# Layer 1's gate projection by seven block products for every eight, with VectorE and ScalarE carrying the partial sums

## The chip, the cores and the metric

The kernel runs on one core of a Trainium2 chip. The metric is the device time of one execution in microseconds (us), lower being better: the median of several runs. The time before is 768.36 us, the median of three runs from 768.17 to 768.40. One core has five engines that matter here, each with an instruction queue of its own: TensorE (PE in the profile, its weight loads are PEld), VectorE (DVE), ScalarE (ACT), GpSimd (POOL) and SyncE (SP), which issues the DMAs.

## The reference, cut to what matters

Two layers work on x, 4 x 512 x 256 in float32. Layer 0 (an mLSTM block, and a feed-forward part with routed low-rank experts) is the same before and after. Layer 1 is:

```python
xn = layernorm(x)
# attention over the four batch entries, causal among them, 16 heads of 16
q, k, v = split(einsum('lne,fe->lnf', xn, weight_qkv), 3)
attn = softmax(where(causal, (q * 16**-0.5) @ k, -inf))
a = (attn @ v) @ weight_out.T
# gated feed-forward part, of every four values the two largest are kept
h = silu(xn @ w_gate) * (xn @ w_up)          # w_gate and w_up: 256 x 1024
f = sparsify_2to4(h) @ w_down
out = x + a + f
```

The attention's sequence is the first axis of x (length 4, B in the code), and it is causal: position l = 0 sees itself alone, so its result is its own v whatever its q is.

## The kernel before

The 512 positions are cut into four row blocks (j = 0 to 3, NJ = 4) of 128 positions for each of the 4 batch entries; a row block is thus 512 rows, and its normed rows lie transposed in `xnT`, two tiles of 128 x 512 (k = 0, 1, the halves of the 256 features).

What layer 1 does for one row block:

- `front_rows(j)`: layernorm statistics on VectorE, one power on GpSimd (`rstd`), the norm on VectorE (`xn`), eight TensorE transposes (`pt`), two ScalarE copies into `xnT`.
- `attention_rows(j)`: for each l, TensorE forms q and k in one product of 512 columns (`qk_ps`) and v in one of 256 (`v_ps`); ScalarE copies them out. `attend_rows` has GpSimd multiply (`pd`), VectorE reduce (`sc`, `st`, `o`), ScalarE take the exponential (`sc`); then eight transposes of `o` (`pt`) and two ScalarE copies (`oT`).
- `rows(j)`: for each of 8 chunks of 128 hidden values, a gate product `gp` and an up product `up`, each of 512 columns and two k. ScalarE applies silu to `gp` (into `hs`), VectorE multiplies `up` into `hs`.
- `sparsified(j, hs)`, once for every four chunks: ScalarE takes absolute values (`hm`), VectorE makes comparisons (`c...`, `rest`, `t...`, `keep`) and multiplies the mask into `hs`. The steps are handed out one by one, with other work between them.
- `finish_rows(j)`: the output products `yp`, 40 of 256 columns for a block, VectorE's addition to x, and the DMA out.

Every float32 matrix product stands in the trace as two passes, each with a weight load of its own. A product of 512 columns and two k is four MATMUL records, one of 256 columns is two records for each k.

The order on each queue is fixed when the program is built. Each part above is a generator (a stream) that yields the time at which its next step could go; `Flow` keeps a cost estimate for every engine (`Clock`) and lets the stream run that is ready first. An engine's queue is strictly in the order in which the steps were handed out, and a step that must wait holds what stands behind it on its engine. PSUM is eight banks (`mm_ps`), each a tile of 128 x 512; `clock.held` marks a bank that may not be given away yet. Nearly all instructions are issued through one helper, so they carry the line number L221 and are told apart by their tiles.

Weights of layer 1 take over buffers of layer 0: `f_gate` lies in the buffer `wguT`, `f_up` in `lora`, `f_down` in `w_gate`, the attention's weights in `WdT` and `w_out`. In the profile they bear these names. The front of row block 0 (`front_rows(0)`) runs inside layer 0's end.

Of the kernel before, what the change touches and what calls it, by code (L numbers as in the profile page):

```python
# [9 lines left out]
AF = mybir.ActivationFunctionType  # L10
# [17 lines left out]
FAR = 3.0e4  # L28
BANKS = 8
AHEAD = 4  # L30


@with_exitstack
def layers_kernel(ctx: ExitStack, tc: tile.TileContext, io: dict, out: bass.AP):
# [193 lines left out]
    class Flow:  # L228
# [34 lines left out]
        def spare(self):  # L263

            return max(clock.free["dve"], self.now + 0.2)

        def wait(self, *aps, banks=0, over=False):

            while True:
                t = clock.ready(*aps, reads=over)  # L270
                room = clock.room(banks) if banks else 0.0
                if room > 1e8:
                    room = self.soon()
                yield max(t, room)
                if not banks or clock.room(banks) <= self.now:
                    return
# [201 lines left out]
    def project(ps, w, xT, lo, n):  # L478

        for k in range(KD):  # L480
            mm(ps[0:n, :], w[:, k, lo : lo + n], xT[:, k, :], start=(k == 0), stop=(k == KD - 1))

# [898 lines left out]


    qkvT = weight("qkvT", 3 * D, "WdT", NFC * D)
    f_gate = weight("f_gate", FF, "wguT", 4 * DFF)
    f_up = weight("f_up", FF, "lora", 2 * DFF + NFC * E * R)
    f_down = weight("f_down", D, "w_gate")
    aoT = weight("aoT", D, "w_out")


    with ExitStack() as l1:
# [3 lines left out]

        def attend_rows(j, q, k, v):

            sc = new(sm, [P, B, B, AH], "sc", 2)
            pool.memset(sc, LOWEST)  # L1400
            for l in range(B):
                m = l + 1
                pd = new(wk1, [P, B, D], "pd", 2)
                pool.tensor_tensor(
                    out=pd[:, 0:m, :], in0=k[:, 0:m, :],
                    in1=q[:, l : l + 1, :].to_broadcast([P, m, D]), op=ALU.mult)
                yield from flow.wait(pd)
                dve.tensor_reduce(
                    sc[:, l, 0:m, :], pd[:, 0:m, :].rearrange("p m (h d) -> p m h d", d=ADH),
                    AX.X, ALU.add)  # L1410
            st = new(sm, [P, B, AH], "st", 2)
            by_m = sc.rearrange("p l m h -> p l h m")
            dve.tensor_reduce(st, by_m, AX.X, ALU.max)
            stb = st.unsqueeze(2).to_broadcast([P, B, B, AH])
# [7 lines left out]
            for l in range(B):  # L1422
                m = l + 1
                pd = new(wk1, [P, B, D], "pd", 2)
                pool.tensor_tensor(
                    out=pd[:, 0:m, :].rearrange("p m (h d) -> p (m h) d", d=ADH),
                    in0=v[:, 0:m, :].rearrange("p m (h d) -> p (m h) d", d=ADH),
                    in1=sc[:, l, 0:m, :].rearrange("p m h -> p (m h)").unsqueeze(2).to_broadcast(
                        [P, m * AH, ADH]),
                    op=ALU.mult)  # L1430
                yield from flow.wait(pd)
                dve.tensor_reduce(
                    o[:, l, :], pd[:, 0:m, :].rearrange("p m c -> p c m"), AX.X, ALU.add)
            while j >= 2 and j - 2 not in out_of:
                yield flow.soon()
            oT = new(wk1, [P, KD, S], "oT", 2)
            for k in range(KD):
                yield from flow.wait(o, banks=1)
                transposed(lambda l, k: o[:, l, k * P : (k + 1) * P], oT, k)
            outs[j] = oT  # L1440

        def sparsified(j, hs):
# [15 lines left out]
            yield flow.soon()  # L1458
            c0213 = flags(2, "c0213")
            dve.tensor_tensor(c0213, hm[:, 0:2, :], hm[:, 2:4, :], ALU.is_ge)  # L1460
            yield flow.soon()
# [4 lines left out]
            yield flow.soon()  # L1466
# [5 lines left out]
            yield flow.soon()  # L1472
# [5 lines left out]
            yield flow.soon()  # L1478
            for n in range(0, 4, 2):
                dve.tensor_tensor(  # L1480
                    hs[:, n : n + 2, :], keep[:, n : n + 2, :], hs[:, n : n + 2, :], ALU.mult)
                yield flow.soon()
            halves.setdefault(j, []).append(hs)

        def finish_rows(j):
# [40 lines left out]
        def attention_rows(j):  # L1526
            while j not in xTs:
                yield flow.soon()
            xT = xTs[j]
            q, k, v = (new(wk1, [P, B, D], n, 1) for n in "qkv")  # L1530
            for l in range(B):
                for name, lo, n in (("qk_ps", 0, 2 * D), ("v_ps", 2 * D, D)):
                    yield from flow.wait(xT, banks=1)
                    ps = mm_ps(name)
                    for kk in range(KD):
                        mm(ps[:, 0:n], xT[:, kk, l * P : (l + 1) * P], qkvT[:, kk, lo : lo + n],
                           start=(kk == 0), stop=(kk == KD - 1))
                    if lo == 0:
                        act.mul(q[:, l, :], ps[:, 0:D], ADH**-0.5)
                        act.copy(k[:, l, :], ps[:, D : 2 * D])  # L1540
                    else:
                        act.copy(v[:, l, :], ps[:, 0:D])
            yield from attend_rows(j, q, k, v)

        def attention_of_all_rows():
            for j in range(NJ):
                yield from attention_rows(j)

        def rows(j):
            xT = xTs[j]  # L1550
            if j + 1 < NJ:
                flow.add(front_rows(j + 1), 10)
            for f0 in range(0, NF, 4):
                hs = new(wk1, [P, 4, S], "hs", 4)
                gated.setdefault(j, []).append(hs)
                for n in range(4):
# [8 lines left out]
                flow.add(sparsified(j, hs))  # L1565
            flow.add(finish_rows(j), turn=1)

        def all_rows():
            for j in range(NJ):
                flow.until(lambda: j in xTs)  # L1570
                yield from rows(j)
            written.add(NJ - 1)

        flow.add(attention_of_all_rows())
        flow.run(all_rows())
        flow.until(lambda: not flow.streams)


# [38 lines left out]
```

## Time and profile before

| what | value |
|---|---|
| median of 3 runs | 768.36 us |
| profiled execution | 768.07 us, of it 766.4 us in the span |
| TensorE clock granted | 1.0 in the whole span |
| PE busy | 759.7 us, 99% |
| VectorE busy | 466.7 us, 61% |
| ScalarE busy | 224.8 us, 29% |
| GpSimd busy | 161.9 us, 21% |
| layer 1's PE work | from 536.40 us to the last product of `yp` at about 763.2 us |

The span is from the first instruction's start to the last one's end; the 1.7 us that the execution takes beyond it lie around the program. A group's "busy" counts the union of its spans, while the mean duration of one instruction overlaps the next one's start, since matmuls are pipelined. So the pace of TensorE is read from starts, not from durations. An idle time in brackets names what ended it.

### The profile page before, as it was taken

How to read it: one execution, taken by the hardware profiler on the slowest of the kernel's cores; microseconds unless marked ns; L12 is line 12 of the kernel's file. 1: busy time of each engine (PE TensorE's matmuls, PEld its weight loads, DVE VectorE, ACT ScalarE, POOL GpSimd, SP SyncE). 2: the span in 40 equal slices, each digit the busy share in tenths (PEclk: the TensorE clock that was granted, in tenths of full speed). 3: DMA queues.
4: the chain of work that ended last, by engine and by line, in shares of the span. 5: the costliest groups of instructions: out<-in, count | busy, mean ns of one | idle time of the engine just before them, and what ended most of it. 6: DMA issues, size and time to landing. Idle time of an engine off the chain costs nothing.

```text
span 766.4 us, 9748 instructions
## 1 busy us (share of the span) xinstructions
PE 759.7 (99%) x3792; PEld 520.1 (68%) x3792; DVE 466.7 (61%) x1075; ACT 224.8 (29%) x457; POOL 161.9 (21%) x154
## 2 busy tenths in 40 slices
PE   9999999999999999999999999999999999999998
PEld 6776878757677876757777765747545764664487
DVE  6787576756644986554477644341376966934971
ACT  4334134332223343122234122110434324214300
POOL 6230051141041050122030041000333224013100
PEclk9999999999999999999999999999999999999999
DMA  7930000120000210000031110001000000000001
GB/s 239 290 109 1 2 0 1 35 78 0 2 1 1 71 41 1 1 1 1 1 111 55 56 42 14 1 0 56 0 1 0 1 28 1 0 29 0 1 14 42
DMA packets 18959, 25.44 MB, mean 33 GB/s; under 512 B 2784, under 2 KB 12768, under 8 KB 18912
## 3 DMA queue, kind: packets, MB, share of 16 engines
q1 hardware_dynamic: 17824, 24.53, 10.1%
q8 instruction: 30, 0.49, 0.3%
q10 hardware_dynamic: 1088, 0.28, 0.2%
q14 instruction: 17, 0.14, 0.1%
HBM read 22.65 MB, written 2.16 MB: 32 GB/s over the span
## 4 chain that ended last, share of the span: by engine, by line
PE 94%; DVE 5%; issue 0%; ACT 0%; POOL 0%; DVEq 0%; POOLq 0%
PE yp L221 18%; PE chunk L221 17%; PE up L221 14%; PE gp L221 14%; PE acc L221 11%; PE qk_ps L221 4%; PE pt L221 2%; PE vp L221 2%; PE o_ps L221 2%; PE v_ps L221 2%; PE lp L221 2%; PE qk L221 1%; PE sums L221 1%; PE hv L221 1%; PE q_ps L221 1%; DVE sl L221 1%
## 5 line engine op out<-in xcount | busy, mean ns | idle before, releaser
L221 PE MATMUL chunk<-low,lora 128*128 128x256 f32 (+1 forms) x384 | 85.8, 383 | 1.6 <-DVE he_pair L221 1.1
L221 ACT ACTIVATE sl<-chunk 128x256 f32<-128x256 f32 x132 | 50.5, 383 | 122.4 <-PE chunk L221 106.7
L221 PE MATMUL chunk<-xnT,wguT 128*128 128x256 f32 (+1 forms) x384 | 83.2, 383 | 0.0
L221 PEld LDWEIGHTS chunk<-xnT,wguT 128*128 128x128 f32 (+1 forms) x384 | 64.2, 181 | 20.4 <-issue 8.8
L221 PEld LDWEIGHTS chunk<-low,lora 128*128 128x128 f32 (+1 forms) x384 | 63.7, 181 | 17.1 <-issue 4.8
L221 DVE SCALAR_TENSOR_TENSOR sl<-sl,chunk 128x256 f32<-128x256 f32 x132 | 54.7, 415 | 29.9 <-ACT sl L221 29.4
L221 PE MATMUL gp<-featT,w_gate 128*128 128x512 f32 x128 | 60.3, 593 | 0.0
L221 PE MATMUL up<-featT,w_up 128*128 128x512 f32 x128 | 60.3, 593 | 0.0
L221 PE MATMUL gp<-xnT,wguT 128*128 128x512 f32 x128 | 60.2, 592 | 0.0
L221 PE MATMUL up<-xnT,lora 128*128 128x512 f32 x128 | 60.2, 592 | 0.0
L221 PE MATMUL yp<-w_down,hid 128*128 128x256 f32 x256 | 56.6, 379 | 0.0
L221 PE MATMUL yp<-w_gate,hs 128*128 128x256 f32 x256 | 56.1, 379 | 0.0
L221 PEld LDWEIGHTS yp<-w_down,hid 128*128 128x128 f32 x256 | 48.4, 190 | 8.2 <-issue 1.9
L221 PEld LDWEIGHTS yp<-w_gate,hs 128*128 128x128 f32 x256 | 48.6, 190 | 6.6
L221 DVE SCALAR_TENSOR_TENSOR tmp<-tmp,gp 128x512 f32<-128x512 f32 x32 | 22.0, 687 | 43.1 <-ACT tmp L221 43.0
L221 ACT ACTIVATE tmp<-gp 128x512 f32<-128x512 f32 x32 | 19.1, 597 | 91.3 <-PE gp L221 91.3
L221 POOL TENSOR_TENSOR pd<-k,q 128x256 f32<-128x256 f32 (+3 forms) x16 | 24.6, 1535 | 97.9 <-ACT k L221 96.6
L221 PEld LDWEIGHTS gp<-xnT,wguT 128*128 128x128 f32 x128 | 24.2, 190 | 28.8 <-issue 28.0
L221 PEld LDWEIGHTS up<-xnT,lora 128*128 128x128 f32 x128 | 24.2, 190 | 28.4 <-issue 27.5
L221 POOL TENSOR_TENSOR ss<-ss,mhalf 128x32 f32<-128x32 f32 x4 | 22.0, 5500 | 101.0 <-DVE ss L221 101.0
L221 PEld LDWEIGHTS up<-featT,w_up 128*128 128x128 f32 x128 | 24.1, 190 | 27.6 <-issue 26.5
L221 PEld LDWEIGHTS gp<-featT,w_gate 128*128 128x128 f32 x128 | 24.0, 190 | 27.5 <-issue 26.8
(221 smaller groups left out, 1207.0 us busy)
## 6 DMA issues: line engine op xcount, KB each, us to landing
ct<-m_dram SPq DMA_DIRECT2D x8, 1024.0 KB, 7.9
x<-in_x SPq DMA_DIRECT2D x3, 512.0 KB, 9.7
out<-x SPq DMA_DIRECT2D x6, 256.0 KB, 2.1
w_gate<-in_w_gate SPq DMA_DIRECT2D x1, 1024.0 KB, 7.1
w_up<-in_w_up SPq DMA_DIRECT2D x1, 1024.0 KB, 7.7
w_down<-in_w_down SPq DMA_DIRECT2D x1, 1024.0 KB, 10.3
wguT<-in_f_gate SPq DMA_DIRECT2D x1, 1024.0 KB, 4.8
lora<-in_f_up SPq DMA_DIRECT2D x1, 1024.0 KB, 5.0
```

What stands on the lines that cost most here:

```text
L221: return tc.keep_in_program_order(f(*args, **kw))
```

## The change

Layer 0 is left alone, and so are the up product, the sparsification's arithmetic and the output product. Four things change in layer 1:

1. The gate product. A pair of hidden chunks by a row block is a 2 x 2 block product: weights a11, a12, a21, a22 of 128 x 128 (k by chunk) and the halves b11 to b22 of `xnT` (128 x 256). Seven products of sums and differences take the place of eight. GpSimd forms the weights' sides once (`sides`: s1, s2, s4 in new rooms, s3 in place of a21), in buffers that layer 0 leaves. VectorE forms the rows' sides for each block (`other_sides`, tile `xd`). `Sevens.pairs` handles two pairs at once (four chunks, one half of a 512-column bank for each pair), on three banks x, y and z. Between the products, the partial sums go from bank to bank: ScalarE copies x into the bank z, which one product at the start has marked as written; it copies y and x to SBUF (`copied`); VectorE adds a bank to such a copy (`added`, twice in a set); ScalarE applies silu to four results of 512 values.
2. The up product stays full; its four banks of a set are held until silu's two halves are there and VectorE has multiplied (`rest`).
3. Row l = 0 of the attention: no q is formed (its `qk_ps` is 256 columns), no scores; ScalarE copies v to `o`.
4. The order: `front_rows(j+1)` starts 3 us into block j rather than 10 and comes with the block's sides, ahead of other streams (`turn=-2`); so do the attention's inner part and the second part of a set (`last`). `sparsified` hands out its next step when VectorE's queue is nearly empty (`unhurried`).

```diff
+        def unhurried(self):
+            while True:
+                yield max(clock.free["dve"] - LITTLE, self.now + 0.1)
+                if clock.free["dve"] <= self.now + LITTLE:
+                    return
...
+    HALF = S // 2
+    def sides(w, rooms, by):
+        v = w.rearrange("p k (q m c) -> p k q m c", m=2, c=P)
+        for i in range(len(rooms) // 3):
+            q = slice(2 * i, 2 * i + 2)
+            a11, a12, a21, a22 = v[:, 0, q, 0, :], v[:, 1, q, 0, :], v[:, 0, q, 1, :], v[:, 1, q, 1, :]
+            s1, s2, s4 = rooms[3 * i : 3 * i + 3]
+            for o, a, b, op in ((s1, a21, a22, ALU.add), (s2, s1, a11, ALU.subtract),
+                                (a21, a11, a21, ALU.subtract), (s4, a12, s2, ALU.subtract)):
+                by.tensor_tensor(out=o, in0=a, in1=b, op=op)
...
+    def other_sides(xT, t, by):
+        b11, b12, b21, b22 = (xT[:, k, h * HALF : (h + 1) * HALF] for k in range(2) for h in range(2))
+        for n, a, b in ((0, b12, b11), (1, b22, t[:, 0, :]), (2, b22, b12), (3, b21, t[:, 1, :])):
+            by.tensor_tensor(out=t[:, n, :], in0=a, in1=b, op=ALU.subtract)
...
+            def product(ps, m, n, start=False, stop=False):
+                for i in range(2):
+                    mm(ps[:, i * HALF : (i + 1) * HALF], a[m](q0 + i), b[n],
+                       start=start and i == 0, stop=stop and i == 1, skip_group_check=True)
+            def copied(ps):
+                t = self.room()
+                act.copy(t, ps)
+                return t
+            def added(ps, t, m, half):
...
+                    dve.tensor_tensor(t, ps, t, ALU.add)
...
+                    took(m, half, t, lambda: None)
...
+            def first():
...
+                product(x, "a11", "b11", start=True)
...
+                act.copy(z, x)
+                yield 0
+                product(y, "s1", "t1", start=True)
+                t2 = copied(y)
+                yield from read(x)
+                product(x, "s2", "t2")
+                t3 = copied(x)
+                yield clock.ready(z)
+                product(z, "a12", "b21", stop=True)
+                took(0, 0, z, free_z)
+                yield from read(y)
+                product(y, "s4", "b22", stop=True)
+                added(y, t3, 0, 1)
+                kept.extend((x, t2))
+            def last():
+                x, t = kept
+                yield from read(x)
+                product(x, "s3", "t3")
+                added(x, t, 1, 1)
+                yield from read(x)
+                product(x, "a22", "t4", stop=True)
+                took(1, 0, x, lambda: clock.held.discard(x.tensor.name))
...
+    gate_sides = sides(f_gate, rooms[0:6], pool)
...
-            for l in range(B):
+            for l in range(1, B):
...
+            act.copy(o[:, 0, :], v[:, 0, :])
...
-                for name, lo, n in (("qk_ps", 0, 2 * D), ("v_ps", 2 * D, D)):
+                for name, lo, n in (("qk_ps", 0 if l else D, 2 * D if l else D), ("v_ps", 2 * D, D)):
...
+        mm(sevens.z, ident, xTs[0][:, 0, :], start=True, stop=True)
...
-                flow.add(front_rows(j + 1), 10)
+                flow.add(following_rows(j + 1), 3, turn=-2)
...
+                first, last = sevens.pairs(gate_sides, b, f0 // 2, gate)
+                yield from first
+                flow.add(last, turn=-2)
                 for n in range(4):
                     yield from flow.wait(banks=1)
-                    gp = mm_ps("gp")
-                    project(gp, f_gate, xT, (f0 + n) * P, P)
-                    act.activation(hs[:, n, :], gp, AF.Silu)
-                    yield from flow.wait(banks=1)
                     up = mm_ps("up")
-                    project(up, f_up, xT, (f0 + n) * P, P)
-                    dve.tensor_tensor(hs[:, n, :], up, hs[:, n, :], ALU.mult)
+                    project(up, f_up, xTs[j], (f0 + n) * P, P)
...
```

With the change, the order that is built is the same as before on all engines up to layer 1's first product. There, TensorE's queue has for one set (row block 2, first four chunks), in the names of the code: x(a11), y(s1), x(s2), z(a12), y(s4), eight transposes of `o`, x(s3), two `up`, x(a22), two `up`.

More of the change, by code (lines that the diff above doesn't have):

```diff
@@ L30 @@
 AHEAD = 4
+LITTLE = 1.0
 @with_exitstack
@@ L481, in project, with kept @@
             mm(ps[0:n, :], w[:, k, lo : lo + n], xT[:, k, :], start=(k == 0), stop=(k == KD - 1))
+    HALF = S // 2
[8 more added lines that the diff above has]
+                by.tensor_tensor(out=o, in0=a, in1=b, op=op)
+        def kept(n):
+            return lambda q: rooms[q // 2 * 3 + n][:, q % 2, :]
+        return {"a11": lambda q: v[:, 0, q, 0, :], "a12": lambda q: v[:, 1, q, 0, :],
+                "a22": lambda q: v[:, 1, q, 1, :], "s3": lambda q: v[:, 0, q, 1, :],
+                "s1": kept(0), "s2": kept(1), "s4": kept(2)}
@@ new lines, in other_sides, with __init__, pairs, rest @@
+    def other_sides(xT, t, by):
+        b11, b12, b21, b22 = (xT[:, k, h * HALF : (h + 1) * HALF] for k in range(2) for h in range(2))
+        for n, a, b in ((0, b12, b11), (1, b22, t[:, 0, :]), (2, b22, b12), (3, b21, t[:, 1, :])):
+            by.tensor_tensor(out=t[:, n, :], in0=a, in1=b, op=ALU.subtract)
+        return {"b11": b11, "b21": b21, "b22": b22,
+                **{f"t{n + 1}": t[:, n, :] for n in range(4)}}
+    class Sevens:
+        def __init__(self, room):
+            self.room, self.z, self.users = room, mm_ps("z"), 0
+            clock.held.add(self.z.tensor.name)
+        def pairs(self, a, b, q0, took):
+            z, left, kept = self.z, {}, []
+            def product(ps, m, n, start=False, stop=False):
[7 more added lines that the diff above has]
+            def added(ps, t, m, half):
+                left[ps.tensor.name] = True
+                def rest():
+                    yield from flow.wait(ps, t)
+                    dve.tensor_tensor(t, ps, t, ALU.add)
+                    del left[ps.tensor.name]
+                    if m == 0:
+                        clock.held.discard(ps.tensor.name)
+                    took(m, half, t, lambda: None)
+                flow.add(rest(), turn=-2)
+            def read(ps):
+                while ps.tensor.name in left:
+                    yield flow.soon(0.2)
+                yield clock.over(ps)
+            def free_z():
+                self.users -= 1
+            def first():
+                yield from flow.wait(*b.values(), banks=2)
+                x, y = (mm_ps(n) for n in "xy")
+                for ps in (x, y):
+                    clock.held.add(ps.tensor.name)
+                product(x, "a11", "b11", start=True)
+                while self.users:
+                    yield flow.soon(0.2)
+                self.users += 1
+                act.copy(z, x)
[20 more added lines that the diff above has]
+                took(1, 0, x, lambda: clock.held.discard(x.tensor.name))
+            return first(), last()
@@ L1385, in layers_kernel @@
     qkvT = weight("qkvT", 3 * D, "WdT", NFC * D)
-    f_gate = weight("f_gate", FF, "wguT", 4 * DFF)
+    t = new(wts, [P, 4 * DFF], "wguT")
+    f_gate = load(t[:, 0 : KD * FF].rearrange("p (k n) -> p k n", n=FF),
+                  io["f_gate"].rearrange("(k p) n -> p k n", p=P))
     f_up = weight("f_up", FF, "lora", 2 * DFF + NFC * E * R)
@@ L1389, in layers_kernel, with room @@
     aoT = weight("aoT", D, "w_out")
+    rooms = [t[:, KD * FF + i * 2 * P : KD * FF + (i + 1) * 2 * P] for i in range(3)]
+    for name, n in (("wvg", KD * V), ("w_og", KD * D)):
+        t = new(wts, [P, n], name)
+        rooms += [t[:, i : i + 2 * P] for i in range(0, n - 2 * P + 1, 2 * P)]
+    rooms = [t.rearrange("p (q c) -> p q c", c=P) for t in rooms]
+    gate_sides = sides(f_gate, rooms[0:6], pool)
+    t = [new(wts, [P, NF * D], name) for name in ("w_up", "w_down")]
+    copies = [t[i % 2][:, i // 2 * S : (i // 2 + 1) * S] for i in range(8)]
+    def room():
+        copies.append(copies.pop(0))
+        return copies[-1]
     with ExitStack() as l1:
@@ L1397, in attend_rows @@
         def attend_rows(j, q, k, v):
-            sc = new(sm, [P, B, B, AH], "sc", 2)
+            sc = new(sm, [P, B - 1, B, AH], "sc", 2)
             pool.memset(sc, LOWEST)
-            for l in range(B):
+            for l in range(1, B):
                 m = l + 1
@@ L1408, in attend_rows @@
                 dve.tensor_reduce(
-                    sc[:, l, 0:m, :], pd[:, 0:m, :].rearrange("p m (h d) -> p m h d", d=ADH),
+                    sc[:, l - 1, 0:m, :], pd[:, 0:m, :].rearrange("p m (h d) -> p m h d", d=ADH),
                     AX.X, ALU.add)
-            st = new(sm, [P, B, AH], "st", 2)
+            st = new(sm, [P, B - 1, AH], "st", 2)
             by_m = sc.rearrange("p l m h -> p l h m")
             dve.tensor_reduce(st, by_m, AX.X, ALU.max)
-            stb = st.unsqueeze(2).to_broadcast([P, B, B, AH])
+            stb = st.unsqueeze(2).to_broadcast([P, B - 1, B, AH])
             dve.tensor_tensor(sc, sc, stb, ALU.subtract)
@@ L1421, in attend_rows @@
             o = new(wk1, [P, B, D], "o", 1)
-            for l in range(B):
+            act.copy(o[:, 0, :], v[:, 0, :])
+            for l in range(1, B):
                 m = l + 1
@@ L1427, in attend_rows @@
                     in0=v[:, 0:m, :].rearrange("p m (h d) -> p (m h) d", d=ADH),
-                    in1=sc[:, l, 0:m, :].rearrange("p m h -> p (m h)").unsqueeze(2).to_broadcast(
+                    in1=sc[:, l - 1, 0:m, :].rearrange("p m h -> p (m h)").unsqueeze(2).to_broadcast(
                         [P, m * AH, ADH]),
@@ L1457, in sparsified @@
             dve.tensor_tensor(c0123, hm[:, 0:4:2, :], hm[:, 1:4:2, :], ALU.is_ge)
-            yield flow.soon()
+            yield from flow.unhurried()
             c0213 = flags(2, "c0213")
             dve.tensor_tensor(c0213, hm[:, 0:2, :], hm[:, 2:4, :], ALU.is_ge)
-            yield flow.soon()
+            yield from flow.unhurried()
             rest = flags(2, "rest", 1)
@@ L1465, in sparsified @@
             dve.tensor_tensor(d30, hm[:, 3, :], hm[:, 0, :], ALU.is_gt)
-            yield flow.soon()
+            yield from flow.unhurried()
             t03, t21 = flags(2, "t03", 1), flags(2, "t21", 1)
@@ L1471, in sparsified @@
                 t21, c0213, rest[:, 0:1, :].to_broadcast([P, 2, S]), ALU.add)
-            yield flow.soon()
+            yield from flow.unhurried()
             keep = new(wk1, [P, 4, S], "keep", 2, BF)
@@ L1477, in sparsified @@
                 dve.tensor_tensor(keep[:, n, :], t, other, op)
-            yield flow.soon()
+            yield from flow.unhurried()
             for n in range(0, 4, 2):
@@ L1481, in sparsified @@
                     hs[:, n : n + 2, :], keep[:, n : n + 2, :], hs[:, n : n + 2, :], ALU.mult)
-                yield flow.soon()
+                yield from flow.unhurried()
             halves.setdefault(j, []).append(hs)
@@ L1537, in attention_rows @@
                            start=(kk == 0), stop=(kk == KD - 1))
-                    if lo == 0:
-                        act.mul(q[:, l, :], ps[:, 0:D], ADH**-0.5)
-                        act.copy(k[:, l, :], ps[:, D : 2 * D])
+                    if lo < 2 * D:
+                        if l:
+                            act.mul(q[:, l, :], ps[:, 0:D], ADH**-0.5)
+                        act.copy(k[:, l, :], ps[:, n - D : n])
                     else:
                         act.copy(v[:, l, :], ps[:, 0:D])
-            yield from attend_rows(j, q, k, v)
+            flow.add(attend_rows(j, q, k, v), turn=-2)
+            while j not in outs:
+                yield flow.soon()
         def attention_of_all_rows():
@@ L1547, in attention_of_all_rows, with room_of_sides, following_rows @@
                 yield from attention_rows(j)
+        bs = {}
+        sevens = Sevens(room)
+        mm(sevens.z, ident, xTs[0][:, 0, :], start=True, stop=True)
+        def room_of_sides():
+            return new(wk1, [P, 4, HALF], "xd", 2)
+        def following_rows(j):
+            yield from front_rows(j)
+            bs[j] = other_sides(xTs[j], room_of_sides(), dve)
         def rows(j):
-            xT = xTs[j]
             if j + 1 < NJ:
-                flow.add(front_rows(j + 1), 10)
+                flow.add(following_rows(j + 1), 3, turn=-2)
+            b = bs[j]
+            while j >= 2 and j - 2 not in out_of:
+                yield flow.soon(0.2)
             for f0 in range(0, NF, 4):
@@ L1555, in rows, with part, gate @@
                 gated.setdefault(j, []).append(hs)
+                there, done = set(), set()
+                def part(m, half, hs=hs):
+                    return hs.rearrange("p (i m) n -> p i m n", m=2)[
+                        :, :, m, half * HALF : (half + 1) * HALF]
+                def gate(m, half, t, free, part=part, there=there):
+                    act.activation(part(m, half), t.rearrange("p (i n) -> p i n", i=2), AF.Silu)
+                    there.add((m, half))
+                    free()
@@ L1556, in rows, with then @@
+                def then(hs=hs, done=done, n=2 * j + f0 // 4):
+                    while len(done) < 4 or sum(map(len, halves.values())) < n:
+                        yield flow.soon()
+                    yield from sparsified(j, hs)
+                first, last = sevens.pairs(gate_sides, b, f0 // 2, gate)
+                yield from first
+                flow.add(last, turn=-2)
                 for n in range(4):
                     yield from flow.wait(banks=1)
-                    gp = mm_ps("gp")
@@ L1559, in rows @@
-                    project(gp, f_gate, xT, (f0 + n) * P, P)
-                    act.activation(hs[:, n, :], gp, AF.Silu)
-                    yield from flow.wait(banks=1)
                     up = mm_ps("up")
-                    project(up, f_up, xT, (f0 + n) * P, P)
-                    dve.tensor_tensor(hs[:, n, :], up, hs[:, n, :], ALU.mult)
-                flow.add(sparsified(j, hs))
+                    project(up, f_up, xTs[j], (f0 + n) * P, P)
+                    clock.held.add(up.tensor.name)
@@ new lines, in rest @@
+                    def rest(n=n, up=up, hs=hs, there=there, done=done):
+                        while (n % 2, 0) not in there or (n % 2, 1) not in there:
+                            yield flow.soon(0.2)
+                        yield from flow.wait(up, hs[:, n, :])
+                        clock.held.discard(up.tensor.name)
+                        dve.tensor_tensor(hs[:, n, :], up, hs[:, n, :], ALU.mult)
+                        done.add(n)
+                    flow.add(rest(), turn=-2)
+                flow.add(then(), turn=-1)
@@ L1566, in rows @@
             flow.add(finish_rows(j), turn=1)
         def all_rows():
+            bs[0] = other_sides(xTs[0], room_of_sides(), dve)
             for j in range(NJ):
-                flow.until(lambda: j in xTs)
+                while j not in bs:
+                    yield flow.soon(0.2)
                 yield from rows(j)
             written.add(NJ - 1)
+        flow.add(all_rows())
         flow.add(attention_of_all_rows())
-        flow.run(all_rows())
         flow.until(lambda: not flow.streams)
```

## The prediction

> **What bounds the kernel now.** I read the page first (busy shares, then the chain of work that ended last), then the chain in order of time for the pace of each kind of product.
>
> ```profile
> PE 759.7 (99%) x3792; PEld 520.1 (68%) x3792; DVE 466.7 (61%) x1075; ACT 224.8 (29%) x457; POOL 161.9 (21%) x154
> PE 94%; DVE 5%; issue 0%; ACT 0%; POOL 0%; DVEq 0%; POOLq 0%
> ```
>
> ```profile
> 509.02 1.72 PE gp L221 x4
> 510.73 1.72 PE up L221 x4
> 522.75 13.81 PE yp L221 x64
> ...
> 728.67 34.55 PE yp L221 x160
> ```
>
> TensorE is the bound, and it is dense: a product of 512 columns and two k takes 1.717 us (0.429 us a pass), 160 passes of 256 columns take 34.55 us (0.2159 each). So half the columns cost half the time. I checked layer 1 by adding up its work: `qk_ps` 16 x 1.717 = 27.5, `v_ps` 16 x 0.863 = 13.8, `gp` and `up` 64 x 1.717 = 109.9, `yp` 320 x 0.2159 = 69.1, 56 transposes x 0.107 = 6.0, together 226.3 us. From 536.56 to 763.22 us there are 226.7. Layer 1 holds 0.4 us of waits, so here TensorE work that goes shortens the run unless a new wait takes its place.
>
> The timeline at layer 1's start gives the hand-over and GpSimd's room:
>
> ```profile
> 538.12 1.03 PE L221 MATMUL v_ps<-WdT,xnT 128*128 128x256 f32 x4
> 538.98 1.88 PE L221 MATMUL qk_ps<-WdT,xnT 128*128 128x512 f32 x4
> 539.09 0.72 POOL L221 TENSOR_TENSOR pd<-k,q 128x256 f32<-128x256 f32 x1 [49.44 <-ACT k L221]
> 539.18 0.37 ACT L221 COPY v<-v_ps 128x256 f32<-128x256 f32 x1 [0.17 <-PE v_ps L221]
> ```
>
> `v_ps` gives way to the next product at 538.98 and ScalarE starts at 539.18: a reader starts 0.20 us after a product's slot. The costs of what reads a bank, from layer 1's groups by shape (ns of one behind the busy time):
>
> ```profile
> L221 ACT COPY oT<-pt 128x512 f32<-128x512 f32 x8 | 4.3, 592 | 0.1
> L221 DVE TENSOR_TENSOR hs<-up,hs 128x512 f32<-128x512 f32 x32 | 21.9, 684 | 28.2 <-PE up L221 22.3 <-ACT hs L221 4.8 <-ACT hm L221 1.2
> ```
>
> The one place in layer 1 where TensorE visibly waited gives the way back:
>
> ```profile
> 717.35 1.91 DVE L221 TENSOR_REDUCE o<-pd 128x256 f32<-128x1024 f32 x1
> 718.75 1.33 PE L221 MATMUL pt<-ident,o 128*128 128x128 f32 x8
> 719.32 0.53 PEld L221 LDWEIGHTS pt<-ident,o 128*128 128x128 f32 x5 [0.31 <-DVE o L221]
> ```
>
> VectorE ends at 719.26, the weight load starts at 719.32: 0.06 us, and the load's own time comes on top (0.19 us for a float32 128 x 128).
>
> **The change, part by part: TensorE.** Gate: 4 row blocks x 2 sets x 7 products x 2 pairs = 112 products of 256 columns, 224 passes x 0.2159 = 48.4 us, in place of 32 x 1.717 = 54.9: -6.6. First row's q: 4 blocks x 2 k x 2 passes = 16 passes, -3.5. The product that marks bank z: two passes of 512, +0.9. The up product, `yp` and the transposes keep their counts. Sum -9.2 us.
>
> [...]
>
> **GpSimd and VectorE ahead of the first set.** The weights' sides are 8 GpSimd operations of 128 x 256, by the `pd` row 0.72 us each, 5.8 us. They stand behind layer 0's last power and ahead of layer 1's. `f_gate` is issued at 416.0 and lands 4.8 us later, and GpSimd idles 49.4 us up to 539.09: hidden, cost 0; without that gap the first y would wait up to 5.8 us. The first block's sides on VectorE (4 x 0.42, by `sc<-sc,st`) come after the last addition to x (536.60 to 537.29) and end near 539; the first set starts at about 547.5: 0. The next block's norm, formerly later, now stands ahead of the attention's reductions on VectorE and its power (1.01 us) ahead of `pd` on GpSimd. My walk ends that `xn` near 544.2, 1.6 us before its transposes, but pushes the first block's `o` to 561.7, against the fourth transpose's slot at 561.8: 0 to 1 us, taken 0.4.
>
> **The hand-overs in a set.** Set row block 2's first set at zero when x(a11) starts; a product takes 0.86. ScalarE copies x to z from 1.06 to 1.66; y(s1) ends at 1.73, and x(s2) may load weights at 1.72 and run at 1.91: 0.18 lost. y's copy runs 1.93 to 2.52. x(s2) ends at 2.77 (its copy 2.97 to 3.57), z(a12) at 3.64, y(s4) at 4.50, eight transposes at 5.36, x(s3) at 6.22, all with their copies long over. VectorE adds y at 4.7 and x from 6.42 to 7.10; two `up` (3.43 us) stand between x(s3) and x(a22), so x(a22) wants its bank at 9.66 and has 2.5 us to spare. Hence one just-in-time wait a set, in the six sets where nothing stands between y(s1) and x(s2) (two have qkv products there): 6 x 0.18 = 1.1. No row has a ScalarE write into PSUM; its nearest is the same copy to SBUF, 0.592. If it were free, the wait goes (0); if double, 6 x 0.6 = 3.6 more. I take the row. ScalarE must not be late there: its queue also has the exponentials and their table loads (1.28 us each); walking block 1's first set, where the exponential stands ahead of x's copy, that copy ends at 6.6 and x(s3) wants it at 8.
>
> [...]
>
> Added loads off the path: VectorE gets 16 additions x 0.684 and 16 differences x 0.425, loses eight l = 0 reductions (3.3) and a quarter of the score operations (2.6): +11.8 on 156 us. ScalarE gets 24 copies x 0.592, four copies of v for four scalings: +14 on 75. Against 219 us of TensorE that is 77% and 41%. Behind the last `up`, TensorE has as before 17.3 us of block 2's `yp`, 3.5 of block 3's attention and 6.9 of its first half; VectorE's remaining masks and additions end about 20.6 us after it, 7 us before the second half needs them. The tail (additions, DMA) is unchanged.
>
> **The sum.** 768.07 - 9.2 + 1.1 + 0.4 = 760.4 against the profiled execution; the median of the runs is 0.3 above that: **760.7 us**. Bounds: no wait at all, and the present 0.4 gone, 768.07 - 9.6 = 758.5; above, each of 48 hand-overs (six a set: two fresh banks, x(s2), y(s4), x(s3), x(a22)) 0.14 late, between the 0.06 of release alone and 0.25 with the load: 6.7, 765.6.
>
> **The rivals.** (1) Every hand-over leaves its weight load bare: 48 x 0.19 = 9.1 us, 768.0, no change. For it: each is a semaphore on TensorE's queue, which before had banks to run ahead. Against: the waits in `gp` and `up` that were over in time cost nothing. 4%.
>
> (2) Slower: VectorE's queue holds x(a22). Its cover is 3.43 - 0.20 - 0.68 = 2.55 us; beyond that TensorE stands still, while the banks are held. A `hs<-up` before ran at 731.75, 3.0 us after its product. Half of a sparsification (two `c` 2.4, `rest` 1.3, `t` 1.4, `keep` 1.6, masks 2.4, half is 4.5) ahead of each addition costs (4.5 - 2.55) x 8 = 15.6, thus 776. It decides from 3.5 us late in every set. For it: VectorE at 77%, in strict order. Against: in the built order most additions have one or two steps ahead of them; the one with a whole sparsification ahead (block 0, second set) has qkv products to cover it, by my walk with 1.8 us left. 9%.
>
> (3) Slower: short passes pay for their loads. A load of 0.190 leaves 0.026 in a pass of 0.216; if half of each load stayed bare on 224 passes, 21.3 us, 780. Against: `yp`'s 160 passes without a gap. 1%. [...]
>
> That fewer products are not in fact issued is excluded by the built queue (28 in each block).
>
> **How the numbers follow.** Forecast 86%, (1) 4%, (2) 9%, (3) 1%. The forecast's own bounds, 758.5 to 765.6, hold over 8 in 10, so they are the range. About 0.2%, or 1.5 us, is what a measurement of this kernel can tell from no change. All of the forecast's range is below 766.8: faster 0.86, same 0.04, slower 0.10.
>
> **What would show it.** `gp` gone, x, y and z with 224 passes and two of 512 at z; starts 0.86 us apart for a product; layer 1's TensorE work about 217 us and its idle 1 to 2 us, mostly at x(s2), released by ScalarE's copy to z. Wrong if the idle before x(a22) is released by VectorE for microseconds (2), if TensorE waits at GpSimd's sides, or if passes of x and y start more than 0.22 us apart with no release named (3).

## The result, and the profile after

The changed kernel takes 759.77 us (median of four runs, 759.73 to 760.13), the kernel before on the same chip 768.33 us (four runs, 768.17 to 768.40). The ratio is 0.989, 95% interval 0.9873 to 0.9907: faster by 8.6 us.

The profiled execution is the one of 760.13 us; in it layer 0, which is the same work, ended 0.47 us later than in the trace of before. So the change is read from layer 1 alone. From its first product's start to its last addition's start it took 226.84 us before (536.40 to 763.24) and takes 218.43 us after (536.87 to 755.30): 8.41 us less.

The page after, busy shares and the shares of the chain that ended last:

```profile
PE 751.7 (99%) x3890; PEld 539.0 (71%) x3890; DVE 490.0 (65%) x1099; ACT 234.9 (31%) x479; POOL 163.4 (22%) x154
PE 91%; DVE 7%; ACT 1%; issue 0%; POOL 0%; DVEq 0%; POOLq 0%
```

TensorE has 98 more instructions and 8.0 us less busy time: more products of half the columns. VectorE gained 23.3 us, which is twice what was forecast, and ScalarE 10.1 us.

The chain in order of time (start, duration, what), with the first set of row block 0:

```profile
537.04 0.86 PE z L222 x2
548.32 0.86 PE x L222 x4
549.18 0.86 PE y L222 x4
550.05 0.99 PE x L222 x4
...
553.63 3.43 PE up L222 x8
557.06 0.86 PE x L222 x4
...
720.73 34.55 PE yp L222 x160
```

The first line is the marking of bank z. A gate product (four passes of 256 columns) has a slot of 0.86 us; x(s2), the third product, has 0.99 us. That 0.13 us is the just-in-time wait behind ScalarE's copy to z. x(a22) follows its two `up` at once, and `yp` is what it was.

In the list of waits of TensorE's weight loads (total us, times, longest us) in layer 1, leaving out "issue", these two are the largest that are more than the ordinary gap between two loads:

```profile
PEld x L222 <- ACT z L222: 1.2, 5, 0.3
PEld pt L222 <- DVE o L222: 0.4, 1, 0.4
```

These totals count all idle time of the weight-load row. The product slots show what TensorE lost by them: 0.63 us at x(s2) in six sets (0.13, 0.12, 0.12, 0.07, 0.07, 0.12), 0.10 us at block 0's transposes of `xn`, 0.33 us at block 2's transposes of `o`. With the TensorE work of 217.1 us, 1.1 us of layer 1 are idle; before, 0.4. (What is left of the 218.43 us, 0.2 us, lies between the last product and the last addition.)

### The profile page after: what moved, and what is told of

It is laid out like the page before. It is cut to its first block, busy times and chain, and to the rows that moved or that the text cites. A ratio compares the mean times of both kernels' runs of the same rounds, so it can differ in the third digit from the quotient of the medians.

```text
span 758.4 us, 9984 instructions
## 1 busy us (share of the span) xinstructions
PE 751.7 (99%) x3890; PEld 539.0 (71%) x3890; DVE 490.0 (65%) x1099; ACT 234.9 (31%) x479; POOL 163.4 (22%) x154
## 3 DMA queue, kind: packets, MB, share of 16 engines
q1 hardware_dynamic: 17824, 24.53, 10.2%
## 4 chain that ended last, share of the span: by engine, by line
PE 91%; DVE 7%; ACT 1%; issue 0%; POOL 0%; DVEq 0%; POOLq 0%
PE chunk L222 18%; PE yp L222 16%; PE up L222 15%; PE acc L222 11%; PE gp L222 7%; PE x L222 3%; PE qk_ps L222 3%; PE pt L222 2%; PE vp L222 2%; PE o_ps L222 2%; PE lp L222 2%; PE v_ps L222 2%; PE y L222 2%; PE qk L222 1%; PE sums L222 1%; PE hv L222 1%
## 5 line engine op out<-in xcount | busy, mean ns | idle before, releaser
L222 PE MATMUL up<-xnT,lora 128*128 128x512 f32 x128 | 58.4, 592 | 0.0
L222 PE MATMUL acc<-WdT,hid 128*128 128x256 f32 (+1 forms) x192 | 41.1, 382 | 0.0
L222 PE MATMUL acc<-tmp,lora 128*128 128x512 f32 x80 | 40.4, 595 | 0.0
L222 POOL TENSOR_TENSOR pd<-k,q 128x512 f32<-128x512 f32 (+2 forms) x12 | 23.3, 1944 | 70.7 <-ACT k L222 44.1
## 6 DMA issues: line engine op xcount, KB each, us to landing
w_down<-in_w_down SPq DMA_DIRECT2D x1, 1024.0 KB, 10.2
```

What stands on the lines that cost most here:

```text
L222: return tc.keep_in_program_order(f(*args, **kw))
```

## The experiments

"Layer 1" below is the same stretch, first product to last addition, in each kernel's profile. All ratios are to the kernel before.

### The parts by themselves

**Gate products and new order, the first row's q and scores as before.**

```diff
-            for l in range(1, B):
+            for l in range(B):
...
-                for name, lo, n in (("qk_ps", 0 if l else D, 2 * D if l else D), ("v_ps", 2 * D, D)):
+                for name, lo, n in (("qk_ps", 0, 2 * D), ("v_ps", 2 * D, D)):
```

> The changed kernel with the first row's attention as before (its q is formed, its scores and its softmax too); the gate by seven products and the order stay. Theory (TensorE's work counts, waits are short): 16 passes of 0.2159 us come back, 759.8 + 3.5 = 763.2 us. Rival (most of the gain is the new order of the streams, or VectorE's relief): q's passes hide in other waits and the time stays within 0.8 us of 759.8.

Measured: 765.24 us (764.98 to 767.81, the two longest with a mean granted clock of 0.998 and 0.997), ratio 0.9972 (0.9958 to 0.9986), layer 1 223.87 us. That is 5.4 us more than the changed kernel. q's work, the theory's 3.5, accounts for 3.45 of it; the rest is one stand of TensorE, a stretch in which it waits. Its timeline:

```profile
595.33 4.30 POOL L222 TENSOR_TENSOR pd<-k,q 128x768 f32<-128x768 f32 x2 [9.50 <-DVE sc L222]
595.70 1.73 DVE L222 TENSOR_TENSOR keep<-t,rest 128x512 bf16<-128x512 bf16 x1
605.47 0.42 ACT L222 ACTIVATE sc<-sc 128x256 f32<-128x256 f32 x1 [2.91 <-DVE sc L222]
605.79 0.57 ACT L222 COPY w_up<-y 128x512 f32<-128x512 f32 x1
606.41 1.13 PE L222 MATMUL y<-xnT,w_og 128*128 128x256 f32 x4 [2.24 <-ACT w_up L222]
```

ScalarE's queue holds the exponential ahead of y's copy and waits 2.91 us for the scores; y(s4) then stands 2.24 us. Two of VectorE's `keep`, ahead of the scores, take 1.73 and 2.57 us beside GpSimd's `pd` (0.41 without it). How much of the lateness is theirs, and how much that of the additional score operations, no run separates. The parts do not simply add up.

**Only the first row's q and scores left out of the kernel before** (the attention part of the diff, nothing else).

> The kernel before with the first row's q, scores and softmax left out, nothing else. Theory: 16 passes less, 768.3 - 3.5 = 764.9 us. Rival (a part of the change that lies beside TensorE's work is what counts): nothing, 768.3.

Measured: 766.56 us, ratio 0.998 (0.997 to 0.9989), layer 1 225.18 us. Of 3.45 us of work gone, 1.66 us arrive. TensorE comes to block 0's transposes of `o` 5.8 us earlier (at 570.94 where it was 576.78), but VectorE's last reduction for them ends only 3.5 us earlier (at 572.48 where it was 575.95):

```profile
572.53 0.53 PEld L221 LDWEIGHTS pt<-ident,o 128*128 128x128 f32 x5 [1.33 <-DVE o L221]
```

**The new order and the first row, with the gate by full products.**

```diff
-            bs[j] = other_sides(xTs[j], room_of_sides(), dve)
+            bs[j] = True
...
+                    gp = mm_ps("gp")
+                    project(gp, f_gate, xTs[j], (f0 + n) * P, P)
+                    act.activation(hs[:, n, :], gp, AF.Silu)
+                    yield from flow.wait(banks=1)
```

> The changed kernel with the gate by full products read by ScalarE as before; no sides are formed, no bank z. The first row's part and the new order of the streams stay. Theory (the order moves nothing): as with the first row's part alone, 764.9 us. Rival (the order itself is a gain): below 764; (the order is a loss that the seven products paid for): above 765.8.

Measured: 764.48 us, ratio 0.9953 (0.9938 to 0.9968), layer 1 223.25 us: its work of 222.85, 0.2 of idle and the 0.2 up to the last addition. The theory's 764.9 came nearly, but it took for granted a saving that the run above did not reach: the new order made the q saving whole, 2.1 us better than that run. From here to the changed kernel, 764.48 to 759.77, or 223.25 to 218.43 in layer 1, is what the seven products bring by themselves: 4.7 to 4.8 us, of work that is 5.7 us less.

### The prices of the sum

**Every gate product of the kernel before as two halves of 256 columns.**

```diff
-                    project(gp, f_gate, xT, (f0 + n) * P, P)
+                    for half in range(2):
+                        c = slice(half * S // 2, (half + 1) * S // 2)
+                        for k in range(KD):
+                            mm(gp[:, c], f_gate[:, k, (f0 + n) * P : (f0 + n + 1) * P], xT[:, k, c],
+                               start=(k == 0), stop=(k == KD - 1))
```

> The kernel before with each gate product as two halves of 256 columns, 256 passes in place of 128, all eight block products. Theory (half the columns cost half the time): 256 x 0.2159 = 55.3 in place of 54.9, 768.7 us. [...]

Measured: 768.38 us, ratio 1.0005 (0.9996 to 1.0014), layer 1 +0.30 us. The chain has the product of eight half passes in the slot that four full passes had:

```profile
547.34 1.73 PE gp L221 x8
```

Half the columns cost half the time here, 0.216 us a pass against 0.43, with a weight load for each. Rival 3 falls: half of each load left bare on these 256 passes would have been some 24 us more (an estimate from the 0.19 us of a load in the trace of before).

**ScalarE's copy to z twice,** the queues' order otherwise the same.

```diff
                 act.copy(z, x)
+                tc.keep_in_program_order(nc.scalar.copy(z, x))
```

> The changed kernel with ScalarE's copy of x into z made twice, the order of the queues as it is otherwise. Theory (x(s2) waits for this copy just in time in six of eight sets, 0.07 to 0.13 us each): the second copy, 0.57 us, lands on TensorE whole in those six, + 3.4, 763.2 us; in the two sets with qkv products between it costs nothing. Rival (TensorE's short waits there come from something else, so the copy has room): 759.8 to 760.5.

Measured: 763.15 us, ratio 0.9935 (0.9922 to 0.9949), layer 1 +3.40 us, which is 6 x 0.57. The second copy is on line 585, and the list of waits names it:

```profile
PEld x L222 <- ACT z L585: 4.2, 5, 0.9
```

So the six x(s2) are just in time, as the walk had it: the 0.57 us more on each copy was 0.57 us more on the path. The list gives five of them to the copy; the sixth, also of 0.9 us, it puts down to GpSimd's `pd`, which ended close by and of which the product reads nothing.

**Bank z marked by one bfloat16 pass of zeros.**

```diff
-        mm(sevens.z, ident, xTs[0][:, 0, :], start=True, stop=True)
+        mm(sevens.z, mark, mark.unsqueeze(1).to_broadcast([P, B, P]), start=True, stop=True)
```

> The changed kernel with bank z marked by one pass of zeros in bf16 in place of two passes in float32. Theory (the marking lies bare on TensorE, 0.86 us in the chain): one pass of 512 columns, 0.43 us, or half of that, is left: 0.4 to 0.65 us less, 759.1 to 759.4 where the changed kernel has 759.8. Rival (the first set waits for its sides or for xn, so an earlier start is lost again): no change, with longer idle ahead of the first transposes or of y.

Measured: 759.63 us, ratio 0.9886 (0.9871 to 0.9901), which these runs can't tell from the changed kernel (layer 1 218.33 against 218.43). The start is 0.6 us earlier, and the transposes of `xn`, which VectorE does not end earlier, take it back: in the list of waits they stand 0.6 us in total behind `xn`. The rival was right.

### How much VectorE may be late

Five, then ten, reads of 256 columns were put on VectorE ahead of the second addition of each set, the one that gives the bank for x(a22). The order on all queues is otherwise the same. The reads start 0.46 us apart; the addition starts 2.17 us after the first of five and 4.46 us after the first of ten.

```diff
+                    if m == 1:
+                        for _ in range(5):
+                            tc.keep_in_program_order(nc.vector.tensor_copy(self.spare, ps[:, 0:HALF]))
                     dve.tensor_tensor(t, ps, t, ALU.add)
```

> The changed kernel with five further VectorE reads of 256 columns of x (0.42 us each, 2.1 us) ahead of the second addition of each set, the order of the queues as it is otherwise. Theory (x(a22) has 2.5 us to spare behind two up products): 759.8 to 761. Rival (VectorE's queue holds TensorE at once): 8 x 2.1, 776.6.

> The same with ten reads, 4.2 us. Theory (cover of 2.5 us, then one for one): (4.2 - 2.5) x 8 = 13.6, 773.4 us, the idle ahead of x(a22) and released by VectorE. Rival (the queues run far enough ahead to take it up, VectorE being at 77% and with this at 93%): 760 to 762. Other rival (no cover): 8 x 4.2, 793.

Measured with five: 767.26 us, ratio 0.9988 (0.9979 to 0.9997), layer 1 +7.14 us. With ten: 790.41 us, ratio 1.0288 (1.0274 to 1.0302), layer 1 +31.4 us. The waits of the first and of the second kernel, in which the ordinary gaps between two loads are counted too:

```profile
PEld x L222 <- DVE w_up L222: 11.4, 8, 2.3
```

```profile
PEld x L222 <- DVE w_up L222: 29.2, 8, 4.5
```

Five reads should have been hidden, and were not; the rival's 776.6 was too much too. Ten reads cost more than the theory's 773.4 and about the 793 of no cover, for another reason. The changed kernel's own trace shows why five were not hidden. From the end of the second addition to the start of x(a22) the eight sets have 1.19, 0.64, 1.34, 1.67, 2.54, 1.60, 1.61 and 1.61 us; the prediction walked one set and found 2.5. The smallest, in block 0's second set:

```profile
572.47 1.85 POOL L222 TENSOR_TENSOR pd<-k,q 128x768 f32<-128x768 f32 x1 [2.58 <-ACT k L222]
572.58 2.02 DVE L222 TENSOR_TENSOR keep<-t,rest 128x512 bf16<-128x512 bf16 x1
...
576.25 0.68 DVE L222 TENSOR_TENSOR w_up<-x,w_up 128x512 f32<-128x512 f32 x1
...
577.57 1.03 PE L222 MATMUL x<-xd,wguT 128*128 128x256 f32 x4
```

In these two runs a wait that is not hidden also costs its hand-over: 0.05 us from the addition's end to the product's start, and a product that is 0.10 us longer (1.13 against 1.03 us). With 2.17 us and this 0.15 more, the lateness over the spares adds to 6.6 us, against 7.1 measured. With 4.46 and 0.15 it is 36.9 - 12.2 = 24.7, which is what the product slots show ahead of x(a22). The 6.7 us that are left of the 31.4 are TensorE's clock, which the windows of the kernel with ten reads show (length, busy time of PE, PEld, DVE, ACT and POOL, granted clock, DMA share, GB/s):

```profile
560.02:563.43 3.41, 3.41 (x6) 2.02 (x7) 2.68 (x4) 1.11 (x2) 2.13 (x2) 0.50 0.00 0
587.33:590.74 3.41, 3.41 (x6) 1.35 (x5) 1.31 (x3) 0.60 (x1) 0.00 (x0) 0.50 0.00 0
611.22:614.63 3.41, 3.41 (x9) 2.68 (x9) 3.41 (x7) 1.17 (x2) 0.00 (x0) 0.50 0.00 0
730.69:734.10 3.41, 3.41 (x5) 1.33 (x4) 1.38 (x3) 0.58 (x1) 0.00 (x0) 0.50 0.00 0
```

Four stretches of 3.41 us at half speed, each behind one of the eight stands, lose 4 x 1.7 = 6.8 us.

### The order

**The first `up` put between y(s1) and x(s2),** to give the copy to z its time.

```diff
                 t2 = copied(y)
+                yield from between()
                 yield from read(x)
```

> The changed kernel with the set's first up product put between y(s1) and x(s2), the planner ordering the rest anew. Theory (the just-in-time waits at x(s2) are most of the 1.1 us that layer 1 idles): they go, 0.6 us less, 759.1 us. Rival (one more bank is held and x(a22) loses cover, so VectorE's additions come late): 759.8 or more, with idle ahead of x(a22).

Measured: 762.06 us, ratio 0.9925 (0.9912 to 0.9937), layer 1 220.67 us, 2.2 us longer. The waits at x(s2) are gone, and others came, which its timeline names:

```profile
642.42 0.53 PEld L222 LDWEIGHTS pt<-ident,o 128*128 128x128 f32 x5 [1.65 <-DVE o L222]
677.83 0.73 PEld L222 LDWEIGHTS x<-xd,wguT 128*128 128x128 f32 x4 [1.04 <-DVE w_up L222]
```

The time went the rival's way, but its reason holds for a small part: of the 3.3 us that TensorE stands in layer 1, 0.5 us is ahead of this x(a22), 2.1 us ahead of block 2's transposes of `o` and 0.5 us ahead of transposes of `xn`. Two `up` still stand between x(s3) and that x(a22). The planner ordered the rest anew, and which of its moves made which wait was not tested.

**The sparsification's steps handed out as before** (`yield flow.soon()` in place of the six `yield from flow.unhurried()`).

> The changed kernel with the sparsification's steps handed out as in the kernel before (each 0.5 us after the other, however long VectorE's queue is). Theory (this part of the order is what leaves VectorE's two additions of a set their 0.6 to 2.5 us to spare): sparsification steps stand ahead of them, x(a22) waits, 1 to 6 us more, 761 to 766, released by VectorE. Rival (the order of these steps does not matter): 759.8.

Measured: 761.44 us, ratio 0.9909 (0.9893 to 0.9926), layer 1 +1.46 us, at the low end of the theory's range. The additions that hand banks back stand behind steps of the sparsification:

```profile
609.76 0.30 PEld L222 LDWEIGHTS up<-xnT,lora 128*128 128x128 f32 x2 [1.58 <-DVE w_down L222]
611.89 0.73 PEld L222 LDWEIGHTS x<-xd,wguT 128*128 128x128 f32 x4 [0.98 <-DVE w_up L222]
```

**The next block's front begun 10 us into a block, and not ahead of others.**

```diff
-                flow.add(following_rows(j + 1), 3, turn=-2)
+                flow.add(following_rows(j + 1), 10)
```

> The changed kernel with the next block's front started 10 us into a block and without precedence, as before. Theory (TensorE's work is the same and the sides are needed a block later only): within 1 us of 759.8. Rival (the sides come late for the next block's first set, or the transposes wait): idle ahead of y or pt, 761 or more.

Measured: 764.21 us (763.19 to 765.51), ratio 0.9946 (0.9931 to 0.9961); its profiled execution is the longest of these, with layer 1 at 223.74 us. The theory, that the start of the front is worth under 1 us, fell. ScalarE's copy to z stands late once, behind an exponential that waits 6.51 us for its scores:

```profile
644.69 1.13 PE L222 MATMUL x<-xd,wguT 128*128 128x256 f32 x4 [2.21 <-ACT z L222]
```

The granted clock is 0.50 from 646.06 to 649.47 us behind it, 1.7 us lost. Two of the four executions, this one among them, have a mean clock of 0.998 and took 765.1 and 765.5 us; the other two have 1.000 and took 763.2 and 763.3. So of the 4.4 us over the changed kernel some 3.5 are there without the clock.

## Why the prediction was right, point by point

The forecast was 760.7 us, with 758.5 to 765.6 as its range; 759.77 came. The mechanism is the one that was given: TensorE bounds layer 1, its work shrinks by 9.2 us, and the new hand-overs give little of it back.

**TensorE's work, -9.2: right.** The slots are 0.86 us for a gate product and for the mark. Short passes cost half (0.216 against 0.43 us in the run with two halves), the first row's q is worth its 3.5 us in the new order (the run with full gate products) and 1.66 us in the old one.

**GpSimd's sides, 0: right.** They ran inside layer 0, from 489.83 to 495.7 us, about 0.75 us each, and GpSimd then idles 45.9 us up to layer 1's first power.

**x(s2), 6 x 0.18 = 1.1: the place right, the size too big; 0.63 came.** In block 2's first set, by the timeline:

```profile
640.93 0.57 ACT L222 COPY z<-x 128x512 f32<-128x512 f32 x1 [8.59 <-PE x L222]
641.55 0.73 PEld L222 LDWEIGHTS x<-xd,wguT 128*128 128x128 f32 x4 [0.20 <-ACT z L222]
641.59 1.09 PE L222 MATMUL x<-xd,wguT 128*128 128x256 f32 x4
```

The copy ends at 641.50, the load starts at 641.55 and the product at 641.59. The term put release (0.06) and a load of 0.19 us behind the copy. Release took 0.05 here (0.11 in block 0's first set). The product's record starts 0.04 us after its load's, while the load is still under way, but the second pass starts only at 641.87, 0.32 us after the load's start, where a pass takes 0.22: about 0.1 of the load's 0.19 us was paid. The copy itself took 0.570 us where 0.592 was assumed, the duration to SBUF. Copies of this shape out of PSUM take 0.570 us to z (mean of eight) in this trace and 0.583 to 0.595 to SBUF (means of four groups), 2 to 4% more; single copies to SBUF take 0.566 to 0.616. The shorter copy does not take the wait away.

**Block 0's `o`, 0.4: a miss in place.** Its transposes had their slot at once (562.22, 0.87 us). About as much fell elsewhere: 0.10 us at block 0's `xn`, which ended at 546.6 where the walk had 544.2, and 0.33 us at block 2's `o`. That the old 0.4 us of waits, left standing in the sum, were gone by the new order makes up most of the rest of the 0.9 us between forecast and median.

**VectorE, +11.8 us: wrong by half.** It is +23.3 us. The additions are as reckoned (16 x 0.68 = 11.0), and the shorter scores save 5.0 rather than 5.9. But the sixteen differences take 10.2 us where 6.8 was given, and work that the change did not touch became longer: `rest` 13.5 us where it had 10.2, `keep` with `rest` 8.2 where it had 6.6, `xn` 7.3 where it had 6.1. The groups by shape after, busy us and ns of one behind the bar:

```profile
L222 DVE TENSOR_TENSOR rest<-hm 128x512 bf16<-128x512 f32 x16 | 13.5, 884 | 0.0
L222 DVE TENSOR_TENSOR xd<-xnT 128x256 f32<-128x256 f32 x8 | 6.2, 776 | 0.0
```

An average duration from the trace of before was taken for operations that the new order puts beside GpSimd's; the last section shows what that does. It cost little here because VectorE is not the bound, but the smallest spare at x(a22) is of this kind: the `keep` shown there took 2.02 us where it takes 0.41 without GpSimd, and the addition stands behind it.

**Rival 2, VectorE holds x(a22): its price was right, its threshold was not.** It was said to decide from 3.5 us late and the cover to be 2.5 us. The runs with reads put ahead show 7.1 us lost at 2.2 us late and the whole gain, and more, lost at 4.5. Between them, by the measured spares and hand-overs, the gain of 8.4 us is gone from about 2.4 us late in every set (an estimate). That no x(a22) waited for VectorE had some luck in it: one set had been walked for all eight, and another had 0.64 us left.

**The order was costed at nothing but 0.4.** By the medians, it is worth 2.1 us to the q saving, the sparsification's steps alone are worth 1.7 us, and the front's start 4.4 us, the clock's part included. That the built order was a good one is thus a condition of the forecast that its sum does not name.

## What to carry to other kernels

Where an engine is dense, as TensorE was here, count its passes: of 9.2 us of work that went from it, 8.4 us came off layer 1, since nearly every new hand-over still had work of TensorE to cover it. The cover is worth reading in every repetition: it was 0.64 us in one set and 2.54 us in another. The order on the other queues is part of such a saving and not decoration: the same 3.45 us of q work left out, with the old rules of order, brought 1.66 us. Where two engines come to work side by side more than before, their operations' old durations may be too short, as those of `rest` were (10.2 us in total before, 13.5 after).

## What the runs showed of the hardware

**Some VectorE operations took longer beside GpSimd's.** A `rest` in the changed kernel that began while a `pd` ran, and two without one, from the timeline:

```profile
568.17 1.73 POOL L222 TENSOR_TENSOR pd<-k,q 128x512 f32<-128x512 f32 x1 [8.31 <-DVE c L222]
568.69 1.75 DVE L222 TENSOR_TENSOR rest<-hm 128x512 bf16<-128x512 f32 x1
...
606.21 1.28 DVE L222 TENSOR_TENSOR rest<-hm 128x512 bf16<-128x512 f32 x2
```

All twelve that ran with GpSimd idle take 0.68 us each (two, overlapping, 1.28). Of the four others, two began just ahead of a `pd` and took 0.68 as well; two began behind its start and took 1.75 and 2.84 us, both ending 0.55 us after GpSimd's operation. The differences `xd` and one `keep` show the same: 0.41 to 0.43 us alone, and 1.09 to 2.02 us for four that overlapped a `pd`, with an end 0.27 or 0.28 us after GpSimd's. `xn` was lengthened as well (0.40 us alone, up to 2.00). It is not so every time: in the trace of before a `rest` that began 0.38 us behind the start of a `pd` took 0.68 us, and that `pd` 2.85. GpSimd's operation was the longer too where the `rest` of 1.75 us ran beside it (`pd` of 512 values 1.73 us here, begun while another `rest` ran, 1.27 at 616.62 with none). Two additions that read PSUM kept their duration beside a `pd`: 0.68 us at 555.03 and 0.67 at 591.33. What ties the two engines together, no run shows.

**Some stands of TensorE were followed by half speed, others as long were not.** A granted clock of 0.50 followed a stand of 2.21 us (front begun later); after one of 2.24 us, in the profiled execution of the kernel with q kept, the clock stayed at 1.00. Two stands of the kernel with ten reads are equally long:

```profile
694.51 1.13 PE L222 MATMUL x<-xd,wguT 128*128 128x256 f32 x4 [2.75 <-DVE w_up L222]
...
729.51 1.13 PE L222 MATMUL x<-xd,wguT 128*128 128x256 f32 x4 [2.75 <-DVE w_up L222]
```

Only the second was followed by half speed. Each of the four drops of that kernel, and the one of the kernel with the front begun later, lasts 3.41 us, and the four begin 8, 7 and 35 times 3.41 us after one another. With the trace of ten reads cut into steps of 3.41 us at the drops' starts, the stands of 3.17, 3.72, 3.01 and 2.75 us that were followed by half speed have 3.17, 2.35, 2.48 and 2.23 us in the step just ahead of the drop; the other four, of 2.67, 1.81, 2.75 and 2.75 us, lie across a border, with at most 1.55 us in one step. The stand of 2.21 us has 2.04 us in the 3.41 us ahead of its drop. So in these two traces the place of a stand in the steps goes with the drop; what sets the steps, no run shows.
